# Gated cross-attention with a mixture of experts: rows turned by VectorE, odd halves in groups of three, idle products and an earlier query step at the start

## The chip, the cores and the metric

The kernel runs on one core of one Trainium2 chip. The metric is device time in microseconds (us) of one execution. TensorE (PE) multiplies matrices, VectorE (DVE) and ScalarE (ACT) work on elements, GpSimd (POOL) issues the gathers and scatters that are addressed by row numbers, SyncE (SP) issues the plain transfers. Each engine works through its own instructions in order.

## What is computed

Eight batches of 512 tokens of 256 numbers go through a gated attention with 16 heads and then through a mixture of 8 experts, of which each token uses two:

```python
x = x + tanh(g_xattn) * attention(layernorm(x), ctx, ctx, mask)
x = x + tanh(g_ffn) * experts(layernorm(x))
...
probs = softmax(x_flat @ router_w + router_b)
top_w, top_idx = top_k(probs, 2)
for e in range(8):
    h = gelu(x_flat @ expert_up[e].T, approximate=False)     # 256 -> 1024
    output += comb[:, e:e+1] * (h @ expert_down[e].T)        # 1024 -> 256
```

The mask keeps a key where it is 1. In these inputs the first 449 keys are masked in every batch, so a window of 128 keys holds all that are kept.

## The kernel before, in words

**Start.** The mask is loaded, compared by DVE (`dropped`, L457) and summed over the rows by four products on PE (`n_ps`, L470). From the sums DVE finds the window of kept keys, and SP then loads that window of the context. Beside this, batch 0 is normalised (L221 to L242, `xn_a`), turned by PE (`xnT_ps`, L281) and multiplied into queries (`q_ps`, L553, two halves of the columns: `queries[0]` and `queries[1]`), and the window into keys and values (`kv_ps` L522, `k_ps` L534). The second query half comes behind the keys. `bqs`, a scaled bias, is made by DVE in L432 ahead of the normalising.

**Attention** (`attend_near`). Batches follow each other, each in 4 groups of heads with 3 slots: scores `t_ps` (L885), their maxima (L890), weights `w_ps` (L915), sums `n_av` (L933), transposes on DVE (L939, L947) and the projection (L954). Between these lie the steps of the batch before: layernorm, router, and writing each routed token into a table in memory that is ordered by expert (`place` L370, `table` L394, eight writes a batch, by POOL). DVE computes from the counts (plan steps, L642 to L692) which group of rows belongs to which expert and at which line of the table it starts.

**Experts.** A job is a group of rows of one expert. Before, a job is a pair (256 rows) or a single (128 rows, what is left of an expert's last pair); `SIZES` counts the jobs that are planned after 3 batches, after 6, and at the end. 32 pairs and 4 singles run as jobs 0 to 35 (the singles as jobs 20, 24, 28, 32); four more singles would run in `compute_extra` only if the routing needed them. A half is 128 rows; there are 68. The steps of a job:

- `list_rows` (L712): SP reads the job's lines of the table into `listed`. `load` (L724, L725): SP loads the expert's two weights, 1 MB each, into one of three buffers.
- `fetch` (L730): POOL gathers the rows, `xg`. `turn` (L746, L748): PE turns them by products with the identity into a PSUM bank, `x_ps`, and DVE copies that to `xT`.
- `go_up` (L758, L762): products `h_ps`, gelu on ACT to `hT`.
- `fetch_y` (L730): POOL gathers what `out` holds for these rows, `y`. It has to wait until the job before has written `out`.
- `go_down` (L776, L779, L782): products `o_ps` per half into one of two banks, DVE adds weight x `o_ps` to `y`, POOL scatters `y` to `out`.

`compute(s)` makes the order of the work around job s: gather for s+2, gather y for s-1, ups of s, turn of s+1, downs of s-1, list of s+3, weights of s+2. That is 11 steps for a pair. Jobs 0 to 3 run inside the attention (`amid`), the others in a loop behind it; in its first jobs one remaining step of the last two batches (a queue: projection, layernorm, router, table writes, plan) is taken after each step. Engines take the work in the order in which the program emits it, unless a scheduler finds another for instructions that aren't pinned by `keep_in_program_order`.

Of the kernel before, what the change touches and what calls it, by code (L numbers as in the profile page):

```python
# [11 lines left out]
F32 = mybir.dt.float32  # L12
# [8 lines left out]
P = 128  # L21
# [14 lines left out]

TOKENS = B * S
GROUP = 2 * P
PAIRS = 2 * TOKENS // GROUP
SINGLES = E  # L40

TABLE = TOKENS // GROUP


PARTS = (3, 6, B, B)
ENDS = [-(-(b * S * 2 - E * (GROUP - 1)) // GROUP) for b in PARTS[:2]] + [PAIRS]
SIZES = [ENDS[0], ENDS[1] - ENDS[0], ENDS[2] - ENDS[1], SINGLES]

OFTEN = SINGLES // 2

TABLES = E * TABLE + SIZES[2]
# [4 lines left out]
for _n in range(SIZES[2]):  # L56
    JOBS.append((2, _n))
    if _n % 3 == 2 and _n // 3 < OFTEN:
        JOBS.append((3, _n // 3))
MAIN = len(JOBS)  # L60
JOBS += [(3, n) for n in range(OFTEN, SINGLES)]
# [3 lines left out]
def flamingo_layer(ctx: ExitStack, tc: tile.TileContext, a: dict, out: bass.AP):  # L65
# [11 lines left out]
    table = tc.dram_tile([TABLES * GROUP, ENTRY], I32, name="table")  # L77

    table_parts = dram_disjoint_views(table, B * QT * 2)
    out_parts = dram_disjoint_views(out, 2)  # L80
# [73 lines left out]
    def clear_table(t):  # L154

        many = t.rearrange("p (n c) -> p n c", c=ENTRY)[:, : TABLES * GROUP // P // 11]
        nc.gpsimd.memset(many, 0)
        nc.gpsimd.memset(many[:, :, 0], TOKENS)
        nc.gpsimd.memset(many[:, :, 1], TOKENS - 1)
        n = many.shape[1]  # L160
        nc.sync.dma_start(
            out=table.rearrange("(p r n) c -> p r (n c)", p=P, n=n),
            in_=t[:, : n * ENTRY].unsqueeze(1).to_broadcast([P, TABLES * GROUP // P // n, n * ENTRY]),
        )
# [8 lines left out]
    full_i = mk.tile([P, 2 * TABLE], I32, tag="full_i", name="full_i")  # L173
    nc.gpsimd.iota(full_i, pattern=[[P, 2 * TABLE]], base=0, channel_multiplier=0)
    full = fixed([P, 2 * TABLE], "full")
# [13 lines left out]
    nc.vector.tensor_scalar(filled, iota, float(TOKENS), None, ALU.mult)  # L189
# [242 lines left out]
    tc.keep_in_program_order(nc.vector.tensor_scalar(bqs, bq, 1.0 / DH**0.5, None, ALU.mult))  # L432
# [13 lines left out]
    with early, tc.tile_pool(name="ps_mask", bufs=1, space=PSUM) as ps_mask:  # L446
# [7 lines left out]
        dropped = mk.tile([P, QT, S], BF16, tag="dropped", name="dropped")  # L454

# [13 lines left out]
        for t in range(QT):  # L469
            nc.tensor.matmul(n_ps, lhsT=ones_b, rhs=dropped[:, t, :], start=(t == 0), stop=(t == QT - 1))  # L470
# [12 lines left out]
        tc.keep_in_program_order(nc.vector.tensor_copy(window_i, window))  # L483
        at = nc.values_load(
# [83 lines left out]
        for step in (*scales, *turns, queries[0]):  # L568
            step()
# [7 lines left out]
        nc.vector.tensor_scalar(eq, keys, here, None, ALU.is_equal)  # L577
        nc.vector.tensor_tensor_reduce(eq, eq, act, scale=1.0, scalar=0.0, op0=ALU.mult, op1=ALU.max, accum_out=kept)
        diag = column("diag", P)
        nc.vector.tensor_scalar(diag, ident, kept, None, ALU.mult)  # L580
# [26 lines left out]
        for step in (keys_values, keys_T, queries[1], keys_less):  # L607
            step()
# [3 lines left out]
    def experts(pool, seen, half_bank, bank, row_bank):  # L612
# [6 lines left out]
        tables, loaded, fetched, turned, made, ys = {}, {}, {}, {}, {}, {}  # L619

        def halves(s):
            return 1 if JOBS[s][0] == 3 else 2

        def plan(k):
            n = SIZES[k]
            single = k == 3
            w = 1 if single else 2
            lines = 2 * TABLE // w

            def planned(shape, name, dtype=F32):  # L630
                return plans.tile(shape, dtype, tag=f"{name}{k}", name=f"{name}{k}")

            def scratch(shape, name):
                return plans.tile(shape, F32, tag=name, name=f"{name}{k}")

            def count():

                count = scratch([P, E], "count")
                nc.vector.scalar_tensor_tensor(count, iota, -float(TOKENS), filled, ALU.mult, ALU.add)  # L642
                if not single:
                    nc.vector.tensor_scalar(count, count, 1.0 - GROUP if k < 2 else -float(P), None, ALU.add)
                more = scratch([P, E, lines], f"more{lines}")
                nc.vector.tensor_tensor(
                    more, count.unsqueeze(2).to_broadcast([P, E, lines]),
                    full[:, ::w].unsqueeze(1).to_broadcast([P, E, lines]), ALU.is_gt,
                )
                groups = scratch([P, E + 1], "groups")  # L650
                nc.vector.memset(groups[:, E:], 0.0)
                nc.vector.tensor_reduce(groups[:, :E], more, AX.X, ALU.add)
                if k:
                    nc.vector.scalar_tensor_tensor(groups, tables["done"], -2.0 / w, groups, ALU.mult, ALU.add)
                ahead = scratch([P, E + 1, E], "ahead")
                nc.vector.tensor_tensor(
                    ahead, lower, groups[:, :E].unsqueeze(1).to_broadcast([P, E + 1, E]), ALU.mult
                )
                begin = scratch([P, E + 1], "begin")
                nc.vector.tensor_reduce(begin, ahead, AX.X, ALU.add)  # L660

                line = scratch([P, E + 1], "line")
                nc.vector.scalar_tensor_tensor(line, iota_e, float(lines), begin, ALU.mult, ALU.subtract)
                if k:
                    nc.vector.scalar_tensor_tensor(line, tables["done"], 2.0 / w, line, ALU.mult, ALU.add)
                past = scratch([P, n, E + 1], f"past{n}")
                nc.vector.tensor_tensor(
                    past, slot[:, :n].unsqueeze(2).to_broadcast([P, n, E + 1]),  # L670
                    begin.unsqueeze(1).to_broadcast([P, n, E + 1]), ALU.is_ge,
                )
                whose = scratch([P, n], f"whose{n}")
                nc.vector.tensor_reduce(whose, past, AX.X, ALU.add)
                whose_i = planned([P, n], "whose_i", I32)
                nc.vector.tensor_scalar(whose_i, whose, -1.0, float(E - 1), ALU.add, ALU.min)
                nc.vector.tensor_tensor(past, past, line.unsqueeze(1).to_broadcast([P, n, E + 1]), ALU.mult)
                far = scratch([P, n], f"far{n}")
                nc.vector.tensor_reduce(far, past, AX.X, ALU.max)
                line_i = planned([P, n], "line_i", I32)  # L680
                nc.vector.tensor_tensor(line_i, far, slot[:, :n], ALU.add)
                tables[k] = (whose_i, line_i, planned([P, n, w, FIELDS], "listed", I32))
                if single:
                    tables["extra"] = planned([P, 1], "extra", I32)
                    nc.vector.tensor_scalar(tables["extra"], begin[:, E:], float(OFTEN), None, ALU.is_gt)
                else:
                    done = planned([P, E + 1], "done")
                    nc.vector.tensor_scalar(done, begin, -1.0, float(n), ALU.mult, ALU.add)
                    nc.vector.tensor_scalar(done, done, 0.0, None, ALU.max)
                    nc.vector.tensor_tensor(done, done, groups, ALU.min)  # L690
                    if k:
                        nc.vector.tensor_tensor(done, done, tables["done"], ALU.add)  # L692
                    tables["done"] = done

            return count
# [11 lines left out]
        def list_rows(s):  # L707
            _, line_i, listed, n = planned_for(s)
            w = halves(s)
            lines = E * 2 * TABLE // w + SIZES[JOBS[s][0]]  # L710
            line = number(line_i, n, lines - 1)
            nc.sync.dma_start(  # L712
                out=listed[:, n],
                in_=table[: lines * w * P].rearrange("(r h p) c -> p r h c", h=w, p=P)[
                    :, bass.ds(line, 1), :, :FIELDS
                ].rearrange("p o h c -> p (o h) c"),
            )
# [16 lines left out]

        def fetch(s):
            xg = gather.tile([P, 2, D], F32, tag="xg", name=f"xg{s}")
            for h in range(halves(s)):
                rows_of(rows, s, h, xg[:, h, :])
            fetched[s] = xg

        def turn(s):
            xg, w = fetched.pop(s), halves(s)
            ps = row_bank(f"x_ps{s}").rearrange("p (c r) -> p c r", c=DC)
            for dc in range(DC):
                for h in range(w):
                    nc.tensor.transpose(ps[:, dc, h * P : (h + 1) * P], xg[:, h, dc * P : (dc + 1) * P], ident)  # L746
            xT = gather.tile([P, DC, GROUP], F32, tag="xT", name=f"xT{s}", bufs=2)
            nc.vector.tensor_copy(xT[:, :, : w * P], ps[:, :, : w * P])  # L748
            turned[s] = xT

        def go_up(s, f):
            up, xT, n = loaded[s][0], turned[s], halves(s) * P
            if f == 0:
                made[s] = hpool.tile([P, FC, GROUP], F32, tag="hT", name=f"hT{s}")
# [688 lines left out]
```

## Time and profile before

| | us |
|---|---|
| six runs | 836.08 to 850.77, median 839.64 |
| profiled execution | 839.63 |
| its span, first to last instruction | 837.8 |
| PE busy | 764.0 (91%) |
| DVE busy | 320.6 (38%) |
| POOL busy | 311.7 (37%) |
| ACT busy | 255.0 (30%) |
| moved by DMA | 121.58 MB, mean 145 GB/s |
| x_ps L746, 136 products | 21.7 |
| xT L748, 36 copies | 23.7 |

The mean granted clock of TensorE is 0.963. A line of the costliest groups reads: source line, engine, operation, output <- inputs, partitions x elements, count | busy us and mean ns of one | idle us of the engine just before them, with what ended most of it. In the chain of waits each line is a start, a length and what filled it, followed back from the last instruction. Attention ends and the experts fill PE alone from about 450 us on.

### The profile page before, as it was taken

What the parts mean: (1) busy time and instruction counts of PE and PEld (TensorE: products, weight loads), DVE (VectorE), ACT (ScalarE), POOL (GpSimd) and SP (SyncE); (2) the same over time, 40 slices, a digit from 0 to 9 for tenths busy, and PEclk for the clock granted to TensorE, in tenths of its full rate; (3) what the DMA queues carried; (4) which work ended last, traced back from release to release, by engine and by line L of the source; (5) the groups of instructions that cost most, each with busy time, mean ns of one, the idle gap of its engine ahead of it and who ended that gap; (6) DMA issues with size and microseconds to landing.
All of it is one profiled execution on the core that took longest, in us unless ns stands there. A gap on an engine that the chain in (4) does not pass through costs nothing.

```text
span 837.8 us, 11329 instructions
## 1 busy us (share of the span) xinstructions
PE 764.0 (91%) x4090; PEld 567.8 (68%) x4090; DVE 320.6 (38%) x958; ACT 255.0 (30%) x487; POOL 311.7 (37%) x420
## 2 busy tenths in 40 slices
PE   4989978797999999899996999999999999899992
PEld 1444544444366656668885888888898988789882
DVE  7867895969674565533320011111011001110100
ACT  3554645362645434332311111111111121111210
POOL 2031041415362342635464445343343333533331
PEclk9998998999899989999998999999999999999996
DMA  4700211000743221334548566665675774657611
GB/s 155 253 7 7 76 34 53 27 28 29 263 155 124 93 72 58 109 121 142 164 142 301 163 221 207 205 205 191 204 226 194 240 238 149 228 185 251 198 48 36
DMA packets 87909, 121.58 MB, mean 145 GB/s; under 512 B 16797, under 2 KB 71712, under 8 KB 87840
## 3 DMA queue, kind: packets, MB, share of 16 engines
q1 hardware_dynamic: 75184, 93.44, 33.7%
q0 software_dynamic: 11840, 26.76, 10.5%
q8 instruction: 36, 0.59, 0.3%
q10 hardware_dynamic: 816, 0.53, 0.2%
q14 instruction: 33, 0.27, 0.1%
HBM read 101.05 MB, written 20.17 MB: 145 GB/s over the span
## 4 chain that ended last, share of the span: by engine, by line
PE 28%; DMA 11%; issue 8%; POOL 3%; DVE 0%; SPq 0%; POOLq 0%; DVEq 0%
PE o_ps L776 14%; PE h_ps L758 13%; DMA out<-y,listed 6%; DMA y<-out,listed 4%; POOL y L730 1%; POOL out L782 1%; PE x_ps L746 1%; DMA xg<-rows,listed 1%; POOL xg L730 0%; DVE y L779 0%; DMA table<-entries,place_i 0%; DMA listed<-table 0%; POOL filled L371 0%; POOL place L370 0%; POOLq L782 0%
## 5 line engine op out<-in xcount | busy, mean ns | idle before, releaser
L776 PE MATMUL o_ps<-down,hT 128*128 128x256 f32 x1088 | 245.7, 384 | 10.7 <-DVE y L779 9.4
L758 PE MATMUL h_ps<-xT,up 128*128 128x256 f32 (+1 forms) x1152 | 244.6, 369 | 3.4 <-DMA up<-in_upT 1.7
L776 PEld LDWEIGHTS o_ps<-down,hT 128*128 128x128 f32 x1088 | 206.3, 192 | 43.1 <-DVE y L779 10.4
L758 PEld LDWEIGHTS h_ps<-xT,up 128*128 128x128 f32 x1152 | 208.9, 191 | 34.6 <-issue 5.6
L762 ACT ACTIVATE hT<-h_ps 128x512 f32<-128x512 f32 (+1 forms) x144 | 81.5, 573 | 368.5 <-PE h_ps L758 315.3
L779 DVE SCALAR_TENSOR_TENSOR y<-o_ps,listed,y 128x256 f32<-128x256 f32 x68 | 32.5, 482 | 272.6 <-DMA y<-out,listed 148.9
L730 POOL DMA_INDIRECT y<-out,listed x68 | 66.1, 971 | 164.3 <-DMA out<-y,listed 131.9
L782 POOL DMA_INDIRECT out<-y,listed x68 | 68.8, 1012 | 101.3 <-DVE y L779 73.9
L920 ACT ACTIVATE n_pT<-w_ps 128x512 f32<-128x512 f32 x128 | 68.3, 598 | 55.7 <-PE w_ps L915 34.5
L890 DVE TENSOR_REDUCE tops<-t_ps 128x4 f32<-128x512 f32 x128 | 79.1, 679 | 12.4 <-PE t_ps L885 12.3
L730 POOL DMA_INDIRECT xg<-rows,listed x68 | 64.9, 954 | 41.5 <-issue 18.8
L394 POOL DMA_INDIRECT table<-entries,place_i x64 | 62.7, 980 | 25.9 <-issue 16.5
L748 DVE COPY xT<-x_ps 128x512 f32<-128x512 f32 (+1 forms) x36 | 23.7, 658 | 112.2 <-PE x_ps L746 109.7
L915 PE MATMUL w_ps<-ql,km 32*128 32x512 f32 x256 | 54.1, 675 | 2.1 <-DVE tops L890 2.1
L885 PE MATMUL t_ps<-k,q 32*128 32x256 f32 x512 | 44.5, 409 | 3.9 <-issue 2.0
L885 PEld LDWEIGHTS t_ps<-k,q 32*128 32x128 f32 x512 | 27.0, 186 | 25.2 <-issue 15.9
L954 PE MATMUL proj_ps<-woT,oT 128*128 128x256 f32 x128 | 33.7, 399 | 10.7 <-DVE oT L947 10.7
L939 DVE STREAM_TRANSPOSE raw<-n_av 128x512 f32<-128x512 f32 x32 | 22.8, 713 | 49.8 <-PE n_av L933 28.2
L867 POOL TENSOR_TENSOR x<-x,bo 128x1024 f32<-128x1024 f32 x8 | 18.9, 2372 | 57.1 <-issue 31.8
L933 PE MATMUL n_av<-n_pT,nv 128*32 128x512 f32 x256 | 37.6, 662 | 2.5 <-DVE xT L748 2.4
L954 PEld LDWEIGHTS proj_ps<-woT,oT 128*128 128x128 f32 x128 | 23.3, 193 | 21.3 <-DVE oT L947 12.7
L553 PE MATMUL q_ps<-n_xnT,wqT 128*128 128x512 f32 x64 | 36.6, 700 | 0.8 <-ACT n_xnT L282 0.5
(187 smaller groups left out, 543.2 us busy)
## 6 DMA issues: line engine op xcount, KB each, us to landing
up<-in_upT SPq DMA_DIRECT2D x36, 1024.0 KB
down<-in_downT SPq DMA_DIRECT2D x36, 1024.0 KB
out<-x SPq DMA_DIRECT2D x8, 512.0 KB
rows<-xn_f SPq DMA_DIRECT2D x8, 512.0 KB
x<-in_x SPq DMA_DIRECT2D x7, 512.0 KB
table<-none SPq DMA_DIRECT2D x1, 2288.0 KB
xg<-rows,listed POOLq DMA_INDIRECT x68
y<-out,listed POOLq DMA_INDIRECT x68
```

The costliest lines, as they stand in the source:

```text
L394: nc.gpsimd.indirect_dma_start(out=table_parts[2 * t + i][:, :], out_offset=bass.IndirectOffsetOnAxis(ap=place_i[:, t, i : i + 1], axis=0) ...
L730: nc.gpsimd.indirect_dma_start(out=dst, out_offset=None, in_=src[: seen[JOBS[s][0]], :], in_offset=bass.IndirectOffsetOnAxis(ap=listed[:, ...
L758: nc.tensor.matmul(ps[:, i, :n], lhsT=up[:, dc, (f + i) * P : (f + i + 1) * P], rhs=xT[:, dc, :n], start=(dc == 0), stop=(dc == DC - 1),)
L762: nc.scalar.activation(made[s][:, f : f + 2, :n], ps[:, :, :n], AF.Gelu)
L776: nc.tensor.matmul(ps, lhsT=hT[:, f, h * P : (h + 1) * P], rhs=down[:, f, :], start=(f == 0), stop=(f == FC - 1))
L782: nc.gpsimd.indirect_dma_start(out=out_parts[h][:, :], out_offset=bass.IndirectOffsetOnAxis(ap=listed[:, n, h, 0:1], axis=0), in_=y[:, h, ...
L885: ins = nc.tensor.matmul(ps[j][:, u], lhsT=q[rows_j, c, t * P : (t + 1) * P], rhs=k[rows_j, c], start=True, stop=True)
L890: nc.vector.tensor_reduce(top[:, 2 * tp : 2 * tp + 2, :].rearrange("p t (i x) -> p t i x", i=2)[:, :, :, 32 * j], ps[j], AX.X, ALU.max,)
L915: ins = nc.tensor.matmul(ps[j], lhsT=km[rows_j, c, i, :], rhs=lowered[b, c][rows_j, i, :], start=True, stop=True)
L920: nc.scalar.activation(pT[:, j, :], ps[j], AF.Exp)
L933: ins = nc.tensor.matmul(av[32 * j : 32 * j + 32, :], lhsT=made_of(b)[3][:, 8 * c + 2 * j + r, :], rhs=pT[:, j, :], start=True, stop=True,)
L954: nc.tensor.matmul(ps[:, t - ts[0], :], lhsT=outs[b, c][:, t * P : (t + 1) * P], rhs=w["woT"][:, c, :], start=(c == 0), stop=(c == DC - 1),)
```

## The change

The change has four parts.

1. **Start.** `stay_awake(n)` issues n products of constants whose result nobody reads (128x128 by 128x512, bf16): 26 ahead of `n_ps`, 4 behind it, 6 behind the keys. Both query halves come before the keys. `bqs` is made behind the window. A few small operations are pinned in program order.
2. **Groups.** Singles go. Four jobs are triples (384 rows of one expert), the rest pairs: an expert with an odd number of halves left gets a triple in place of a pair and a single. Main jobs become 32: 28 pairs and 4 triples (jobs 19, 23, 27, 31), again 68 halves. The table has one layout of 33 lines of 128 rows per expert. The plan of the last batch is new (`plan_rest`, some 40 small DVE operations). A triple's products have 384 columns, one chunk to a bank.
3. **Turning.** For jobs 4 to 31, `turn_block` lets DVE transpose 32x32 blocks from `xg` to `xT`, 16 instructions per job of 32 partitions each, with the blocks moved between partition groups. It uses no PE, no bank and no copy. A quarter of it stands behind each of the first four ups of a job; a pair's `compute` has 14 steps.
4. **The last job** does two ups, then the downs of the job before, then its other ups.

```diff
+        stay_awake(26)
...
-        for step in (*scales, *turns, queries[0]):
+        for step in (*scales, *turns, *queries):
...
-        for step in (keys_values, keys_T, queries[1], keys_less):
+        for step in (keys_values, keys_T, lambda: stay_awake(6), keys_less):
...
-SIZES = [ENDS[0], ENDS[1] - ENDS[0], ENDS[2] - ENDS[1], SINGLES]
+SIZES = [ENDS[0], ENDS[1] - ENDS[0], TRIPLES, 2 * TOKENS // GROUP + E - 1 - TRIPLES - ENDS[1]]
+OFTEN = SIZES[3] - 7
...
-for _n in range(SIZES[2]):
-    JOBS.append((2, _n))
-    if _n % 3 == 2 and _n // 3 < OFTEN:
-        JOBS.append((3, _n // 3))
+for _n in range(OFTEN):
+    JOBS.append((3, _n))
+    if _n % 3 == 1 and _n // 3 < TRIPLES:
+        JOBS.append((2, _n // 3))
...
         def halves(s):
-            return 1 if JOBS[s][0] == 3 else 2
+            return 3 if JOBS[s][0] == 2 else 2
...
+        def turn_block(s, i):
+            w = halves(s)
+            if i == 0:
+                where, bufs = (wide[0], 1) if w == 3 else (gather, 2)
+                turned[s] = where.tile([P, DC, w * P], F32, tag="xT" if w == 2 else "xT3", name=f"xT{s}", bufs=bufs)
+            src = fetched[s].rearrange("p h (k g x) -> p g k h x", k=DC, x=32)
+            dst = turned[s].rearrange("p k (h i r) -> p i k h r", h=w, r=32)
+            for g in range(4):
+                nc.vector.transpose(dst[32 * g : 32 * g + 32, i], src[32 * i : 32 * i + 32, g])
...
         def ups(s):
-            return [lambda f=f: go_up(s, f) for f in range(0, FC, 2)]
+            m = 512 // (halves(s) * P)
+            return [lambda f=f: go_up(s, f, m) for f in range(0, FC, m)]
...
-            steps += ups(s)
+            up = ups(s)
+            last = downs(s - 1) if s > first else []
             if s + 1 < end:
-                steps.append(lambda: turn(s + 1))
-            if s > first:
-                steps += downs(s - 1)
+                turned_next = turns(s + 1)
+                for step in up:
+                    steps += [step, *turned_next[:1]]
+                    turned_next = turned_next[1:]
+                steps += turned_next + last
+            else:
+                steps += up[:2] + last + up[2:]
```

The triples' tiles take the memory of two pools of the attention, which are closed when the queue is empty. If the routing needed more than 11 pairs behind the first 17 jobs, `compute_extra` would run three or six further pairs.

## Prediction

> **What bounds the kernel now.** I read the engine table first, then the costliest groups, the chain of waits, and the time lines of PE and DVE where the chain leaves PE. Engine table and groups of the page:
>
> ```profile
> PE 764.0 (91%) x4090; PEld 567.8 (68%) x4090; DVE 320.6 (38%) x958; ACT 255.0 (30%) x487; POOL 311.7 (37%) x420
> L776 PE MATMUL o_ps<-down,hT 128*128 128x256 f32 x1088 | 245.7, 384 | 10.7 <-DVE y L779 9.4
> L758 PE MATMUL h_ps<-xT,up 128*128 128x256 f32 (+1 forms) x1152 | 244.6, 369 | 3.4 <-DMA up<-in_upT 1.7
> L779 DVE SCALAR_TENSOR_TENSOR y<-o_ps,listed,y 128x256 f32<-128x256 f32 x68 | 32.5, 482 | 272.6 <-DMA y<-out,listed 148.9
> ```
>
> PE works 91% of the span and two expert products take 490 of its 764 us. The same table by stretches of time (columns: length, then busy us of PE, PEld, DVE, ACT, POOL, then the clock):
>
> ```profile
> 420.00:470.00 50.00, 41.77 (x190) 35.87 (x189) 6.83 (x22) 5.95 (x11) 26.13 (x27) 0.93 0.61 202
> 470.00:600.00 130.00, 130.00 (x622) 114.62 (x621) 14.92 (x27) 21.95 (x38) 53.26 (x55) 1.00 0.63 205
> 600.00:720.00 120.00, 116.97 (x601) 103.85 (x600) 13.17 (x26) 20.02 (x39) 44.94 (x47) 0.99 0.67 219
> 720.00:815.00 95.00, 95.00 (x464) 83.99 (x463) 10.10 (x20) 15.64 (x28) 37.29 (x38) 0.99 0.54 174
> ```
>
> From 470 on PE is full but for 3 us, and DVE is 11% busy (14.92 of 130). The chain of waits shows the cycle of one job and the two places where PE stood (start, length, what):
>
> ```profile
> 453.18 5.33 DMA y<-out,listed
> 458.59 0.49 DVE y L779
> 459.13 8.84 PE o_ps L776 x32
> 467.96 6.91 PE h_ps L758 x32
> 474.87 0.44 PE x_ps L746 x4
> 475.31 6.91 PE o_ps L776 x32
> ...
> 710.93 5.93 DMA y<-out,listed
> ...
> 717.04 0.49 DVE y L779
> ...
> 717.58 8.86 PE o_ps L776 x32
> ...
> 733.78 3.46 PE o_ps L776 x16
> ...
> 765.52 3.57 PE h_ps L758 x32
> ...
> 820.64 2.82 DMA y<-out,listed
> ```
>
> A job of 256 rows costs PE 6.91 + 0.44 + 6.91 = 14.26 us; one of 128 rows 3.57 + 0.22 + 3.46 = 7.25. Both stalls end with a gather of y from out, which must wait for the job before to have written out. PE's time line puts them at 6.51 us before 459.13 and 2.92 before 717.58, and each is followed by a slow o_ps (8.85 for 6.91: 1.93 lost).
>
> **The change part by part.** *1. x_ps leaves PE.* Jobs 0 to 3 keep it; jobs 4 to 35 were 28 pairs at 0.44 and 4 singles at 0.22, 13.2 us. Behind 467.96 lie the turns of jobs 11 to 35: 21 x 0.44 + 4 x 0.22 = 10.1 us, all on a full PE, so on the path. The 3.1 us of jobs 4 to 10 are counted in part 4. In their place DVE gets 16 stream transposes of 32 partitions x 128 elements per pair (192 per triple). No such row exists. The nearest:
>
> ```profile
> L947 DVE STREAM_TRANSPOSE oT<-n_o 128x512 f32<-128x512 f32 x16 | 11.4, 710 | 0.5
> L748 DVE COPY xT<-x_ps 128x512 f32<-128x512 f32 x32 | 22.0, 687 | 94.7 <-PE x_ps L746 92.2 <-remote 2.5
> L346 DVE MAX8 top<-pr 128x8 f32<-128x8 f32 x32 | 3.6, 154 | 0.4
> ```
>
> Upper bound 0.71 us (four times the elements), lower 0.15 (nearly none). A line between these at 128 elements gives 0.154 + 0.556 x 120/504 = 0.29; I take 0.30. So 4.8 us a pair (bounds 2.4 and 11.4), 0.37 x 16 = 5.9 a triple, less the copy of 0.69 that goes. DVE then does 4.8 + 2 x 0.48 = 5.8 us in a job of 13.82: hidden under the products. Queued behind the transposes on DVE is y of the job before; its first half comes about 4.8 - 3.46 = 1.4 us later, its second not at all, and the bank it frees is wanted a whole job later. With this cover gone all 16 would be on the path, 4.8 us a job. Turned blocks are ready long before h_ps of the next job wants them, since xg is fetched two jobs ahead. POOL's gathers issue while DVE transposes in the trace already: xg at 349.49 took 0.99 beside L947 at 350.04, against a mean of 0.954, so I add nothing for that pair.
>
> The Trainium skill ("VectorE: DVE Perf Modes", section "Rules for kernel authors") speaks against this edit: a 128x128 transpose belongs on TensorE where PSUM will do as its place, since DVE turns only 32x32 blocks. Followed, it would keep part 1's 10.1 us on the path. The trace agrees that PE is the quicker at it (0.44 us for four squares, against 4.8 by my bounds), but the rule counts the operation alone, and here PE is full and DVE empty.
>
> *2. Four triples for four singles.* Columns multiplied stay (68 halves: 32 x 2 + 4 before, 28 x 2 + 4 x 3 after), so no matmul time changes: 7.25 + 14.26 before, 10.37 + 10.37 after without the turns. What goes is four rounds of gather, add and scatter, and 4 x 2 MB of weights. From one y gather to the next the pair jobs took 12.08 (492.23 to 504.31) to 14.57 us, mean 13.87 over nine: POOL issues six gathers or scatters of about 1.28 = 7.7, and waits 4.7 to 7.6 for landings. A single gave PE 7.25 us of cover for such a round; therefore the chain of waits runs through out and y from 597 to 717 and ends in the stall of 2.92 us. A triple needs 9 x 1.28 + 7.6 = 19.1 us and covers 20.7. So the stall and its slow o_ps go: 2.92 + 1.93 = 4.9 us (bounds 0 and 4.9). Planning adds some 40 small DVE operations at 0.15 to 0.29 us, 6 to 12 us spread over routing of the last batch, when DVE is idle; they delay nothing but job 17 onwards, which is 100 us away.
>
> *3. The start.* PE's time line at the start (the columns are start, busy us, instruction, idle before):
>
> ```profile
> 9.03 2.40 PE L470 MATMUL n_ps<-dropped,ones_b 128*128 128x512 bf16 x4 [9.03 <-DVE dropped L457]
> 12.62 2.08 PE L281 MATMUL xnT_ps_a<-ident,xn_a 128*128 128x128 f32 x8 [1.20 <-ACT xn_a L271]
> 15.16 3.77 PE L553 MATMUL q_ps<-n_xnT,wqT 128*128 128x512 f32 x4 [0.46 <-ACT n_xnT L282]
> 21.88 1.88 PE L553 MATMUL q_ps<-n_xnT,wqT 128*128 128x512 f32 x4
> 24.59 1.15 PE L885 MATMUL t_ps<-k,q 32*128 32x256 f32 x16 [0.82 <-ACT q L557]
> ```
>
> The first q_ps run at half the speed of the second. With a warm PE: xnT_ps 1.0 and q_ps 1.9 less, while the second q_ps (1.88) moves ahead of the keys and their chain, which it lengthens, and off the wait before t_ps. Keys then decide: t_ps at about 22.3 instead of 24.59, 2.3 us gained. Bounds: 0 where the keys' chain (DVE pick at 19.52, k) alone decides, and a loss: 26 idle products at n_ps's 0.59 cold would end at 1.1 + 15.3 = 16.4, 7 us behind n_ps's 9.03; all at half of that they end at 8.7. I take the quick side, as records of 0.59 for a lone product hold its fill. The moved bqs sat in front of BN statistics, where DVE waited 2.28 us for bq; the mask, not that, sets dropped. The attention stage is 90 to 95% PE, so the gain carries.
>
> The Trainium skill ("TensorE: Matmul & The Clock Gate", Part 1) gives half clock until about 3.4 us of sustained work, and back after an idle window of that length. The trace's 2.92 us idle at 714.66 already brought the slow o_ps: by the page's window part 2 would be 2.92, by the row it is 4.9. No row shows idle products; by the page's rates 26 of them end near 9 us, an estimate.
>
> *4. The hand-over, 380 to 468.* 14 steps a job empty the queue of routing sooner than 11, so SP reads job 7's list behind all eight table writes of batch 6, and on DVE job 7's transposes stand ahead of both y of job 4, job 9's ahead of those of job 6. Before, those y ran at 392.92 and 396.39, and xg(7) was gathered from 400.00 to 402.24. Landing some 2 us later, it would let y(4) run at about 404: PE, whose logits of batch 7 wait for DVE and its bank, stands from 397 to 404, 7 us, and a slow product of 1.93 may follow. The table writes of batch 7 (8 x 1.28 = 10.2 on POOL) then come in one piece ahead of out(5), which delays y(6) but leaves y(8) about where it was. Against this go the old stall and slow o_ps, 6.51 + 1.93 = 8.4, and 3.1 of x_ps: 3.1 + 8.4 - 8.9 = 2.6 us gained. Bounds: -8, where y(6) makes PE stand as long again, and +11.5, where no new stall comes.
>
> *5. The end.* The last y gather waits for out of job 34 and landed at 823.5, behind the last o_ps at 822.2; with downs(34) after two ups it lies under some 8 us of h_ps. out then starts 0.9 us after o_ps, not 3.4: 2.5 us less (bounds 0 and 2.5).
>
> Sum: 10.1 + 4.9 + 2.3 + 2.6 + 2.5 = 22.4 us from the profiled 839.63 (span 837.8, 1.8 around it), which is the median's 839.64: **817.2 us**.
>
> **Rivals.** *(a) The round of y and out becomes the bound.* A pair now covers 13.82, the mean round is 13.87, and weights come denser. Then part 1 gains nothing in 25 jobs: 817.2 + 10.1 = 827. For: the chain is on that path from 597 to 717. Against: rounds of 12.08 exist, so the mean holds PE's own pace. *(b) The hand-over loses.* DVE's transposes for a late xg hold up y twice (7 and 8 us) and nothing recovers: part 4 is -8, 10.6 worse than taken, 828; with the 4.9 of part 2 not won either, 833. For: SP already waits 37.5 us for table writes. *(c) Slower: DVE becomes the bound.* It decides once 16 transposes and two y pass 14.26, at 0.83 us each. At 0.90 (the 0.71 row and 3 us of POOL's gathers waited for in each job), 16 x 0.90 + 0.96 = 15.4, 1.6 over the plan in 25 jobs: 817 + 40 = 857. Against: 128 elements for 512. *(d) It doesn't do what it says:* more than 11 pairs left starts three extra jobs, 3 x 13.82 and about 10 to refill: 868. I counted the reference's routing: halves per expert 6, 9, 6, 10, 8, 9, 11, 9, which needs four triples and exactly 11 pairs.
>
> **How the numbers follow.** Forecast 0.57, (a) 0.17, (b) 0.15, (c) 0.07, (d) 0.02, below 806 (part 4 at +11.5 and a start above 2.3) 0.02. The forecast's own range is 808 (part 4 at +11.5) to 824 (parts 3 and 2 at 0); to hold 8 in 10 it goes up through (a) and (b): 806 to 834. A measurement here tells 0.5% from no change (835.4 to 843.8): faster 0.86, same 0.05 (a bad (b)), slower 0.09.
>
> **What would show it.** Right: no x_ps after 430, h_ps and o_ps alternating at 13.82 a pair with PE full from 470, transposes near 0.30 in DVE's rows, first q_ps at 1.9 and t_ps near 22.3, no stall of PE behind y after 600, last out 0.9 us behind the last o_ps. Wrong: transposes over 0.8, PE waiting for DVE xT or for y between 470 and 800, or n_ps later than 9.5. Most open is where PE stands from 390 to 460.

## Result and profile after

The changed kernel took 879.52 us (median of 20 runs) against 841.18 (46 runs of before): 1.0477 times as long, 95% interval 1.0452 to 1.0503. Here and below a ratio is estimated from the undisturbed runs of both kernels, and it can differ by up to 0.4% from the quotient of the medians (1.0456 here). The prediction, 817.2 us, was wrong in its sign. The profiled execution took 879.55 us, its span 877.8.

Engine table and groups of the page of the changed kernel (as shown of before: busy us, count, mean ns, idle before and what ended it):

```profile
PE 777.6 (89%) x3878; PEld 553.7 (63%) x3878; DVE 440.3 (50%) x1384; ACT 255.6 (29%) x487; POOL 312.7 (36%) x420
L888 PE MATMUL o_ps<-down,hT 128*128 128x256 f32 x1088 | 252.5, 391 | 40.3 <-DVE y L891 40.3
L859 DVE STREAM_TRANSPOSE xT<-xg 32x128 f32<-32x128 f32 (+1 forms) x448 | 139.9, 312 | 205.7 <-DMA xg<-rows,listed 160.1
L894 POOL DMA_INDIRECT out<-y,listed x68 | 68.6, 1009 | 165.6 <-DVE y L891 140.3
```

x_ps is gone from PE's costliest groups (jobs 0 to 3 keep it), and the transposes cost what was forecast. But PE now stands 40.3 us in front of o_ps (10.7 before), and what it waits for is DVE's y. DVE in turn stood 160 us in front of transposes, waiting for gathered rows. DVE is busy for half of the span (50%); what delays y is that DVE waits.

The same stretches as before (length, then busy us of PE, PEld, DVE, ACT, POOL, then the clock):

```profile
20.00:340.00 320.00, 292.94 (x1744) 159.00 (x1743) 223.19 (x640) 154.10 (x311) 97.57 (x156) 0.91 0.26 84
...
470.00:600.00 130.00, 123.27 (x570) 107.85 (x569) 55.74 (x172) 21.19 (x36) 52.78 (x54) 0.99 0.61 203
600.00:720.00 120.00, 104.99 (x432) 84.47 (x432) 38.88 (x116) 17.41 (x32) 43.05 (x44) 0.94 0.47 150
720.00:815.00 95.00, 78.69 (x327) 65.00 (x328) 32.16 (x92) 13.48 (x24) 32.66 (x34) 0.89 0.47 156
```

PE, full there before but for 3 us, is empty for 6.7, 15 and 16.3 us, and the granted clock falls with it (0.99, 0.94 and 0.89). The same landmarks in both traces say where the 39.9 us of span came in (start of the first t_ps, of the first o_ps of job 0, of h_ps of job 10; end of the last o_ps; end of the span):

| stretch, us | before | after | change | forecast |
|---|---|---|---|---|
| to the first t_ps | 24.6 | 21.6 | -3.0 | -2.3 |
| t_ps to job 0 | 228.9 | 236.8 | +7.9 | 0 |
| job 0 to h_ps of job 10 | 214.3 | 217.0 | +2.7 | -2.6 |
| h_ps of job 10 to the last o_ps | 354.4 | 386.5 | +32.1 | -15.0 |
| last o_ps to the end | 15.6 | 15.8 | +0.2 | -2.5 |

The fourth row holds the result. PE's time line there, the rows where it stood:

```profile
600.85 8.86 PE L888 MATMUL o_ps<-down,hT 128*128 128x256 f32 x32 [6.63 <-DVE y L891]
...
651.07 5.89 PE L888 MATMUL o_ps<-down,hT 128*128 128x256 f32 x16 [9.90 <-DVE y L891]
...
727.42 5.27 PE L888 MATMUL o_ps<-down,hT 128*128 128x256 f32 x16 [9.79 <-DVE y L891]
...
800.51 6.26 PE L888 MATMUL o_ps<-down,hT 128*128 128x256 f32 x16 [7.70 <-DVE y L891]
```

The first lies in front of job 17, the other three inside the o_ps of the triples 19, 23 and 27. The products behind each run slowly: 16 of them take 5.3 to 6.3 us where 3.5 is their time, and the first 32 take 8.86 where 6.9 is. The cause is in DVE's time line, two rounds long (an operation's row, and in brackets the idle time before it and what ended it):

```profile
596.50 3.77 DVE L859 STREAM_TRANSPOSE xT<-xg 32x128 f32<-32x128 f32 x12 [12.18 <-DMA xg<-rows,listed]
600.31 0.48 DVE L891 SCALAR_TENSOR_TENSOR y<-o_ps,listed,y 128x256 f32<-128x256 f32 x1
...
602.12 0.48 DVE L891 SCALAR_TENSOR_TENSOR y<-o_ps,listed,y 128x256 f32<-128x256 f32 x1
615.84 3.77 DVE L859 STREAM_TRANSPOSE xT<-xg 32x128 f32<-32x128 f32 x12 [13.23 <-DMA xg<-rows,listed]
619.64 0.48 DVE L891 SCALAR_TENSOR_TENSOR y<-o_ps,listed,y 128x256 f32<-128x256 f32 x1
```

and in POOL's for the same round:

```profile
602.88 1.00 POOL L894 DMA_INDIRECT out<-y,listed  x1 [0.79 <-DVE y L891]
606.10 0.98 POOL L823 DMA_INDIRECT y<-out,listed  x1 [2.22 <-DMA out<-y,listed]
607.38 0.97 POOL L823 DMA_INDIRECT y<-out,listed  x1 [0.30 <-issue]
608.66 0.95 POOL L823 DMA_INDIRECT xg<-rows,listed  x1 [0.30 <-issue]
609.92 0.95 POOL L823 DMA_INDIRECT xg<-rows,listed  x1 [0.30 <-DMA y<-out,listed]
620.40 1.02 POOL L894 DMA_INDIRECT out<-y,listed  x1 [9.54 <-DVE y L891]
```

These are the rows of job 21, gathered behind y of job 17, and on DVE the turn of job 21 stands in front of the adds of job 17. So one round runs in series: from y's first add both halves of out go (3.6 us), out lands (2.2), y and xg are gathered (4.8), xg lands (5.0), twelve transposes (3.8), and y is added again. From 600.31 to 619.64 that is 19.33 us, for a job that takes PE 13.8. In this stretch four other transposes stand between the two adds of a job.

In the program the turn of job j+2 comes before the adds of job j. In the built order it stands further forward: to j+3 among the pairs (limited by the two buffers of xT, of which the turn can use one only when h_ps of job j+1 is done), and to j+4 around the triples, whose xT has a buffer of its own. A triple also takes no turn in the pairs' two buffers, so the pair behind it finds one free a job sooner: job 21 takes that of job 18. The trace has j+4 in front of the adds of jobs 15 to 17, 19 to 21, 23 to 25 and 27. With j+3 the rows were gathered a round earlier: the transposes of jobs 13 to 18, from 496 to 565 us, each start when an h_ps ends, not when rows land, and PE is full at 13.81 us a job from 482 to 579.

### The profile page after: what moved, and what is told of

It reads as the page before. It is cut to its first block, busy times and chain, and to the rows that moved or that the text cites. A ratio compares the mean times of both kernels' runs of the same rounds, so it can differ in the third digit from the quotient of the medians.

```text
span 877.8 us, 11223 instructions
## 1 busy us (share of the span) xinstructions
PE 777.6 (89%) x3878; PEld 553.7 (63%) x3878; DVE 440.3 (50%) x1384; ACT 255.6 (29%) x487; POOL 312.7 (36%) x420
## 5 line engine op out<-in xcount | busy, mean ns | idle before, releaser
L888 PE MATMUL o_ps<-down,hT 128*128 128x256 f32 x1088 | 252.5, 391 | 40.3 <-DVE y L891 40.3
L888 PEld LDWEIGHTS o_ps<-down,hT 128*128 128x128 f32 x1088 | 212.1, 196 | 80.3 <-DVE y L891 44.6
L859 DVE STREAM_TRANSPOSE xT<-xg 32x128 f32<-32x128 f32 (+1 forms) x448 | 139.9, 312 | 205.7 <-DMA xg<-rows,listed 160.1
L870 PEld LDWEIGHTS h_ps<-xT,up 128*128 128x128 f32 x1024 | 195.0, 192 | 44.8 <-DVE oT L1080 2.3
L396 POOL DMA_INDIRECT table<-entries,place_i x64 | 62.5, 977 | 24.2 <-issue 16.8
L1048 PE MATMUL w_ps<-ql,km 32*128 32x512 f32 x256 | 59.3, 726 | 2.0 <-DVE tops L1023 1.9
L1087 PE MATMUL proj_ps<-woT,oT 128*128 128x256 f32 x128 | 36.3, 423 | 8.5 <-DVE oT L1080 8.5
L1066 PE MATMUL n_av<-n_pT,nv 128*32 128x512 f32 x256 | 40.4, 708 | 2.4 <-DVE xT L847 2.3
L568 PE MATMUL q_ps<-n_xnT,wqT 128*128 128x512 f32 x64 | 32.9, 641 | 1.8 <-ACT k L555 0.9
```

The costliest lines, as they stand in the source:

```text
L396: nc.gpsimd.indirect_dma_start(out=table_parts[2 * t + i][:, :], out_offset=bass.IndirectOffsetOnAxis(ap=place_i[:, t, i : i + 1], axis=0) ...
L859: nc.vector.transpose(dst[32 * g : 32 * g + 32, i], src[32 * i : 32 * i + 32, g])
L870: nc.tensor.matmul(ps[:, i, :], lhsT=up[:, dc, (f + i) * P : (f + i + 1) * P], rhs=xT[:, dc, :], start=(dc == 0), stop=(dc == DC - 1),)
L888: nc.tensor.matmul(ps, lhsT=hT[:, f, h * P : (h + 1) * P], rhs=down[:, f, :], start=(f == 0), stop=(f == FC - 1))
L1048: ins = nc.tensor.matmul(ps[j], lhsT=km[rows_j, c, i, :], rhs=lowered[b, c][rows_j, i, :], start=True, stop=True)
L1087: nc.tensor.matmul(ps[:, t - ts[0], :], lhsT=outs[b, c][:, t * P : (t + 1) * P], rhs=w["woT"][:, c, :], start=(c == 0), stop=(c == DC - 1),)
```

## Experiments

Four kernels each ran on one chip with the kernel before, whose median was 821.47 us for e1 to e4, 838.87 for e5 to e8 and 838.98 for e9 to e12. Ratios to it are compared, not times. "Main stretch" below is that from h_ps of job 10 to the last o_ps, as in the table, and "hand-over" that from job 0 to h_ps of job 10. Each stretch is read from one profiled execution. The attention (t_ps to job 0) took 218 to 223 us on the chip of e1 to e4 and 231 to 236 on the other two; the main stretch, where PE is full at a clock of 1.00 unless it waits, is what is compared between chips.

**e1, transposes in program order.**

```diff
-                nc.vector.transpose(dst[32 * g : 32 * g + 32, i], src[32 * i : 32 * i + 32, g])
+                tc.keep_in_program_order(
+                    nc.vector.transpose(dst[32 * g : 32 * g + 32, i], src[32 * i : 32 * i + 32, g])
+                )
```

> The changed kernel with one edit: each DVE transpose is kept in program order, so the turn of job j+2 (not j+3 or j+4) stands in front of y of job j. Theory A (the transposes stand too early on DVE, wait there for a row gather that POOL issued only just before, and y, out and the next gather of y wait behind them): PE's 40.3 us of idle behind y fall under 12, the half-clock stretches behind them go, 825 us (815 to 838). Rival B (the triples do it: three gathers a round and one buffer each for their xg, xT, hT and y): the stalls around jobs 19, 23 and 27 stay, 865 to 880. Rival C (the idle products at the start bring a lower clock through the attention): only the part behind 420 improves, and the windows from 20 to 340 keep a clock near 0.91.

Measured 812.55 us, ratio 0.9856 (0.979 to 0.9923); on the scale of the change's own runs (841.18 before) that is 829 us, inside theory A's range. Page and windows of e1:

```profile
L890 PE MATMUL o_ps<-down,hT 128*128 128x256 f32 x1088 | 243.4, 382 | 1.0 <-DVE y L893 1.0
...
470.00:600.00 130.00, 130.00 (x588) 111.43 (x588) 54.56 (x168) 23.02 (x40) 58.46 (x60) 1.00 0.63 207
600.00:720.00 120.00, 120.00 (x526) 99.64 (x525) 47.39 (x142) 22.17 (x40) 50.90 (x54) 1.00 0.60 194
```

One pin takes the stall behind y from 40.3 us to 1.0, with the triples, their single buffers and three gathers a round unchanged. Rival B falls. The main stretch is 338.5 us against 354.4 before and 387.7 on this same chip in e4, which leaves the order to the scheduler. Rival C, as the cause of the loss, falls too: the clock from 20 to 340 was 0.97 here with the idle products, as in e3 and e4 without them, and e4 below loses as much with the old start.

**e2, PE turns all rows; pairs, triples, start and last job as changed.**

```diff
-            return [lambda i=i: turn_block(s, i) for i in range(4)]
+            return [lambda: turn(s)]
...
-                for step in up:
-                    steps += [step, *turned_next[:1]]
-                    turned_next = turned_next[1:]
-                steps += turned_next + last
+                steps += up + turned_next + last
```

> The changed kernel, but PE turns the rows of all jobs as before (a triple in two banks one after the other), pairs, triples and start as changed. Theory A: no transposes in front of y, so no stalls behind y beyond those of before; with 10 to 13 us of products for the turns 828 to 842. Rival B: stalls around the triples stay, 865 or more.

816.28 us, ratio 0.9926 (0.9897 to 0.9954), which is 835 on that scale and inside theory A's range; PE is full from 470 and the main stretch is 348.6. So the turn on DVE, in order, is worth 348.6 - 338.5 = 10.1 us there. Against the profile of before the triples are worth 354.4 - 348.6 = 5.8; but e11 below, with the pairs and singles of before and PE's turn, had no stall behind 470 and took 349.2, while e8 and e12, with the same jobs, took 353.6 and 353.0. The triples are worth the stall where it comes, and 0.6 us where it doesn't.

**e3, the kernel before with DVE's turn,** left to the scheduler:

```diff
-            steps += ups(s)
-            if s + 1 < end:
-                steps.append(lambda: turn(s + 1))
+            up = ups(s)
+            if s + 1 < end:
+                for step, block in zip(up, turns(s + 1)):
+                    steps += [step, block]
+            else:
+                steps += up
```

> The kernel before (pairs and singles, old start), jobs from 4 on turned by DVE as in the change, in the order the scheduler finds (the turn of job j+3 in front of y of job j). Theory A: a single leaves PE 7.2 us of cover for a round that now holds the row gather's landing and 4.8 us of transposes, so rounds near the singles grow to 17 or 19 us and PE stands there: 845 to 875. Rival B: without triples the turn on DVE only gains its 10 to 13 us: 825 to 832.

823.55 us, ratio 1.0006 (0.997 to 1.0043). Both expectations missed. Without triples the turn never stands further forward than j+3, and the main stretch is 349.6, as long as with PE's turn and no stall (349.2 in e11). PE stands 6.7 us behind 470 (3.0 before), all of it in jobs 21 to 27, at singles or next to them. So theory A had the place right and the size wrong: beside singles even j+3 uses up the 10 us that the turn gives PE. A loss like that of the change needs j+4.

**e4, the changed kernel with the start of before** (no idle products, second query half behind the keys).

> The changed kernel with the start as before (no idle products, second query half behind the keys). Theories A and B: 3 us for the start, 878 to 885. Rival C: the clock from 20 to 340 returns from 0.91 to 0.95 and the time falls by 6 to 10, to 870 to 874.

858.6 us, ratio 1.0456 (1.0382 to 1.0531), as the change itself. PE waits 39.8 us behind y, the main stretch is 387.7. On the scale of the change's own runs that is 879.5, inside the range of theories A and B. The start has no visible part in the loss.

**e5, every transpose in program order, at j+3.** The pin is that of e1; behind the ups, `compute` now has:

```diff
+                steps += up
+                if s == first:
+                    steps += turns(s + 1)
+                if s + 2 < end:
+                    steps += turns(s + 2)
+                steps += last
```

> The changed kernel with each transpose kept in program order, but the turn of job j+3 put in front of y of job j for every job, triples too. Theory A, in its sharper form: the loss comes where the turn of job j+4 stands in front of y of job j, because POOL then issues that row gather right behind the gather of y of job j, in the same round, so the round out, y, xg, turn, y, out becomes serial (19.3 us). With j+3 the row gather was issued a round earlier, so there is no such wait: ratio 0.980 to 0.995, PE full from 470 on. Rival D (every transpose that stands ahead of its program place costs, in proportion): ratio 1.005 to 1.03, PE idle behind y 15 to 35 us.

838.35 us, ratio 0.9992 (0.9959 to 1.0025): the ratio was missed by theory A and by D, but the stretch that they were about speaks clearly. The main stretch is 339.9 us, with PE waiting 1.2 us in it. DVE's time line of e5 in a steady round:

```profile
661.26 5.05 DVE L860 STREAM_TRANSPOSE xT<-xg 32x128 f32<-32x128 f32 x16 [5.40 <-DMA xg<-rows,listed]
666.97 0.48 DVE L893 SCALAR_TENSOR_TENSOR y<-o_ps,listed,y 128x256 f32<-128x256 f32 x1 [0.67 <-DMA y<-out,listed]
668.20 0.48 DVE L893 SCALAR_TENSOR_TENSOR y<-o_ps,listed,y 128x256 f32<-128x256 f32 x1 [0.74 <-DMA y<-out,listed]
```

The transposes still wait for rows, but are done before y has landed, so y loses nothing. What e5 loses lies in the hand-over: 226.3 us, against 214.3 before and 210.9 to 216.5 in e6, e7 and e8 on its own chip. Why it is longer is left open.

**e6, as e1, but PE turns jobs 4 to 9.** The edit lets `turns(s)` return `[lambda: turn(s)]` for s below 10, placed behind the ups.

> As e1 (transposes in program order), but PE still turns the rows of jobs 4 to 9; DVE from job 10 on. If e1 lost its missing part in the hand-over (o_ps of job 8 came at 449.5 us there and at 443.5 in e2), this takes e2's way to job 9 and e1's pace behind it: 5 to 7 us under e1, ratio 0.976 to 0.980. If it is lost elsewhere: as e1, 0.984 to 0.987.

822.68 us, ratio 0.9779 (0.9722 to 0.9836), as forecast for a loss in the hand-over, though its interval overlaps that of e1. The main stretch stays at 338.4 and the hand-over is 213.7. On the chip of e1 to e4 the hand-over took 216.1 with pinned transposes (e1), 207.9 with those of the change (e4) and 207.8 with PE's turn (e2): there the pinned order costs some 8 us, by one profile each. e6 and e7 have the same jobs, and their hand-overs differ by 2.8 us.

**e7, as e6 with one If around all extra jobs.**

```diff
-            middle = MAIN + MORE - OFTEN
             with tc.If(any_behind(0) == 1):
-                some(MAIN, middle)
-                with tc.If(any_behind(1) == 1):
-                    some(middle, len(JOBS))
+                some(MAIN, len(JOBS))
```

> As e6, with one If around all extra jobs in place of two nested ones. If the nested If takes the gain of the last job back (the span goes on 13.0 to 14.0 us behind the last out in the changed versions, 11.2 and 11.3 in those with a single If), the end comes 2 to 2.7 us sooner than in e6: ratio 0.973 to 0.977. If not, as e6.

821.69 us, ratio 0.9812 (0.9745 to 0.9878). The span ends 15.7 us behind PE's last product (e6: 15.4): nesting isn't what costs. The ratio lies above both expectations, and its interval overlaps that of e6.

**e8, e11, e12: only the start, on the kernel before.** e8 takes all of it, e11 the idle products and the moved bqs without the query order, e12 the query order and the moved bqs without idle products; e8's edit is that of the change's diff.

> The kernel before with only the start of the change (idle products, both query halves ahead of the keys). My forecast for the start alone, 2.3 us: ratio 0.996 to 0.998, t_ps near 21.6. If the attention doesn't carry the gain on (its waits or slow-clock stretches take it back): 0.999 to 1.002.

> The kernel before with the idle products (26 and 4) and the moved bqs, query halves in the old order. If the idle products cost by a slower clock later in the attention: ratio 1.002 to 1.007, slow-clock stretches between 20 and 340 us of 40 us or more in sum. If the earlier second query half costs: 0.997 to 1.000.

> The kernel before with both query halves ahead of the keys, no idle products. If the idle products are what costs: ratio 0.998 to 1.001. If the query order is: 1.002 to 1.007.

e8: 842.3 us, ratio 1.0043 (1.0015 to 1.0072). e11: 835.18, 0.9938 (0.9899 to 0.9977). e12: 838.6, 0.9999 (0.996 to 1.0039). The first t_ps came at 21.7, 21.2 and 23.6 us (24.6 before), so the idle products do bring it forward by about 3 us. They don't do so each time: with the whole new start it came at 21.5 to 22.0 us in seven profiles and at 24.1 in e10, whose first eight q_ps took 5.40 us (3.70 in the change); with the old start it came at 24.2 to 26.3. What the whole then does differs in sign between e8 and e11, which ran on different chips and are alike but for the query order and six idle products. Half of that (4.4 of some 9 us) lies in the main stretch of their profiles, far behind the start: 353.6 with a stall of 2.8 us in e8, 349.2 without one in e11. e8 lies above both of its expectations and e11 below both of its own, though e11 had the clock that was feared (0.91 from 20 to 340). e12 lies in the first of its ranges, but the reason given there, that the idle products cost, is what e11 speaks against.

**e9, e6 with the start of before.**

> As e6 (transposes in program order, PE turns jobs 4 to 9), with the start as before. If the start of the change costs what e8 showed (ratio 1.0043), this is the quickest version: 0.972 to 0.977. If its 2.9 us are carried on: 0.979 to 0.983.

827.5 us, ratio 0.9847 (0.9789 to 0.9906): above both expectations; its interval overlaps that of e6. Together with e8, e11 and e12 the worth of the start stays unsettled within about 0.7% either way.

**e10, e6 without the code of the extra jobs** (this leaves out a path that other inputs may need; these inputs don't).

> As e6 without the code of the extra jobs, which this routing doesn't need (no branch behind the last job). In all profiles the span ends 14.8 to 15.9 us behind PE's last product, whether the last out goes out 0.9 or 3.4 us behind it. If PE's way through the branch sets the end, that stretch shrinks by 3 us or more, and to the last out's 11 us at most; ratio 0.970 to 0.976. If not, it stays near 15 and the ratio near 0.978.

815.29 us, ratio 0.9701 (0.9635 to 0.9767), as forecast for a branch that sets the end. Time line of the end of e10 and, below it, of e6:

```profile
807.74 2.75 PE L890 MATMUL o_ps<-down,hT 128*128 128x256 f32 x12
...
811.29 0.98 POOL L896 DMA_INDIRECT out<-y,listed  x1 [2.45 <-POOLq L1515]
```

```profile
804.69 2.32 PE L890 MATMUL o_ps<-down,hT 128*128 128x256 f32 x10
...
807.81 0.98 POOL L896 DMA_INDIRECT out<-y,listed  x1 [2.44 <-DVE y L893]
```

Both issue the last out 0.8 us behind PE's last product. e10's span ends at 819.7, e6's at 822.4: 9.2 and 15.4 us behind that product. The branch costs 6 us, by this one pair of profiles, in two parts that the traces show. The landing of the last out is recorded in 16 parts. In e10 all 16 are there 3.3 us behind PE's last product; in e6, with the same issue, 12 are there at 3.1 and the other four come at 4.0 to 5.6, while PE's sequencer is in the branch instruction for 4.83 us (until 5.5) and blocks of instructions are loaded. POOL waits for all 16 in the branch. That is 2.3 us. From the landing to the end of the span it takes 9.8 us in e6 and 5.9 in e10, another 3.9. That the loading of instructions slows the four parts is likely and not shown.

## Why the prediction was wrong, point by point

**Part 1, the turn on DVE: the step that failed.** The price was right: 303 ns for 128 elements and 370 for 192, forecast 0.30 and 0.37. So was the gain on PE, 10.1 us, as e1 against e2 shows. That the price hit so well owes something to luck, as it was a straight line between two rows far from it (0.15 and 0.71). What failed is the step that y's first half comes only 1.4 us later and its second not at all. It charged y with the length of the transposes and put their wait for rows at nothing, on the ground that "xg is fetched two jobs ahead". That read the order off the program. The scheduler's order put the turn of job j+4 in front of the adds of job j around the triples, and its rows were gathered in that same round. Twelve transposes (3.8 us) then stood with a wait of 12 to 13 us in front of y's first add, on the one chain (out, y, out) that sets the pace where PE doesn't. The Trainium skill's rule weighed there ("VectorE: DVE Perf Modes", section "Rules for kernel authors": TensorE for a 128x128 transpose where PSUM will do) would have given e2's 0.9926; in order DVE gave e1's 0.9856 (main stretch 348.6 and 338.5), so the rule isn't what the change fell by. e1 undoes the order alone and takes the ratio from 1.0477 to 0.9856; e5 puts it at j+3 and keeps the main stretch at 339.9. The working of part 4 had this pattern in hand ("job 7's transposes stand ahead of both y of job 4") and charged it there only.

**Part 2, triples.** The forecast was 4.9 us, for a stall of 2.92 us and its slow product; e2's main stretch gives 5.8 against the profile of before. That the stall is there to be won was taken from one execution: e11, with the old jobs, had none and took 349.2, so the gain is 0.6 to 5.8. (Of the nine rounds of before, the longest is 14.52 us, not 14.57.) The triples are also what made the reach of j+4 possible, through their own xT buffer; pairs alone (e3) stay at j+3. That a larger group loosens a buffer limit on which the order rested was in no step. The sum of parts 1 and 2, 15.0 us, measures 354.4 - 338.5 = 15.9 in e1, and 10.7 against e11.

**Part 3, the start.** 2.96 us at the first t_ps, forecast 2.3, with the first q_ps at the 1.9 that was taken. n_ps started at 9.61 us, later than the 9.5 that was set as a sign of being wrong: it stood behind the idle products, and the gain came all the same. That it "carries" was not shown. In the changed kernel's profile the attention took 7.9 us longer for the same work, with a clock of 0.91 from 20 to 340 us against 0.95 (half clock for some 58 us instead of 32, an estimate from these means). It isn't shown that the start caused this: on another chip the same stretch had 0.97 in e1 and in e4, with the new and the old start, and in e5 to e12 lengths from 231.0 to 236.2 us with either.

**Part 4, the hand-over.** Forecast: PE stands 7 us near 396 to 404. PE's time line of the changed kernel:

```profile
396.32 7.17 PE L888 MATMUL o_ps<-down,hT 128*128 128x256 f32 x32
413.57 0.47 PE L330 MATMUL lg_ps<-ident,lgT 128*128 128x128 f32 x1 [10.08 <-DVE y L891]
...
452.92 8.86 PE L888 MATMUL o_ps<-down,hT 128*128 128x256 f32 x32 [2.27 <-DVE y L891]
```

Right place and mechanism, 10.1 us instead of 7, and a stall of 2.27 with a slow o_ps stayed where none was forecast: +2.7 instead of -2.6, inside its bounds. But the +2.7 is small beside what the hand-over does by itself: 209.1 to 216.5 us in e8, e11 and e12, which have the jobs of before (214.3), and 207.9 in e4, which has those of the change.

**Part 5, the end.** The last out was issued 0.8 us behind the last o_ps, as forecast. Nothing came of it, because an out issued earlier didn't land earlier: before, it was issued 3.4 us behind PE's last product and landed at 6.0; in the change it was issued at 0.8 and landed at 5.9. The term of 2.5 us took a landing of the same length for granted. It was 2.6 us before and 5.1 in the change, beside the branch of the extra jobs; without that branch it was 2.5 again (e10).

**Rivals.** (a) didn't happen: in e1 the round follows PE. (b)'s stalls came (10.1 and 2.3 us), but not its price: the hand-over was 2.7 us longer in the two profiles, within its own spread. (c) had the engine right and the mechanism wrong: DVE never lacked time, at 0.30 us and 50% busy; it lacked the rows. A rival "DVE waits in order for a late operand in front of y" was the one to price. (d) didn't happen: 1024 products of h_ps are 32 jobs.

The lowest ratio with the extra jobs kept is that of e6, 0.9779, with an interval that overlaps those of e1, e7 and e9; e10 shows what the branch behind the last job would give back.

## What to carry to other kernels

When work is moved to an idle engine, its busy share says little: an engine that works in order is occupied while it waits for an operand, and whatever stands behind waits too (12 to 13 us a round here, at 50% busy). Read the order in which the built program places the moved instructions, not the order of the source, and for each ask when its operand is issued and what stands behind it; a larger tile or a buffer of its own can let a scheduler pull it further forward. Where early-ready work shares an engine with a link of the critical chain, pin it behind that link.

## What the runs showed of the hardware

With a branch behind the last job the span ended 14.8 to 15.9 us behind PE's last product in all 13 profiles that have it, whether the last out was issued 0.8 or 3.4 us behind, and 9.2 us without the branch (e10). PE's sequencer spent 4.4 to 5.1 us in that branch, and the last out landed at 5.1 to 6.0 us in all 13, against 3.3 without: the outs issued at 0.8 us took 4.2 to 5.1 us to land, the later ones 2.6, and that of e10 2.5.

In the attention the granted clock lay between 0.91 and 0.97 over 320 us, and the stretch took 231.0 to 236.2 us in e5 to e12: kernels with the same attention differed there by more than the 3 us that were worked for at the start. Idle products gave a warm start in most executions and not in all (first t_ps at 21.2 to 22.0 us, once at 24.1).
